# A conditioned residual kernel: other places for two batch-pair products and two rank terms in the order of the output tiles

## The chip, the cores and the metric

The kernel runs on one core of a Trainium2 chip. The metric is the device time of one execution in microseconds, as the median of several runs. A profiled execution is a run of its own: its span goes from the first to the last instruction on the core, and its device time is the span and what lies around it.

## The reference

For each of 8 batches, `x` is a 1024 x 512 matrix and `cond` a vector of 512. Two residual layers follow each other, both with weights that depend on `cond`. Cut to what matters:

```python
h = gelu(layernorm(cond) @ w1 + b1)              # (8, 512)
x_a, x_b = split(h @ w2 + b2)                    # each (8, 512, rank 8)
layer = base_layer[None] + einsum('bdr,bkr->bdk', x_a, x_b)
x = x + (x + einsum('btc,bco->bto', x, layer))   # first layer
ys = cond / sqrt(512)
d = rsqrt(einsum('bi,io->bo', ys * ys, weight * weight) + 1e-8)
x = x + einsum('bsi,io->bso', x * ys[:, None, :], weight) * d[:, None, :]
```

Everything is linear in `x`, so for each batch there is one 512 x 512 matrix Q, and the output is `x[b] @ Q[b]`. With B = base_layer + 2I, and N[b] = I + diag(ys[b]) weight diag(d[b]), Q[b] is B @ N[b] and a term of rank 8 that carries `x_a` and `x_b` through the second layer.

## The kernel before

**Arithmetic.** Each fp32 operand of a large product is split into a high part (a cast on ScalarE) and a low part (a subtraction on VectorE), and each product is done as high x high, high x low and low x high. That is three matmuls for each block of the contraction. An output tile of 128 rows and 512 columns takes 4 x 3 = 12 matmuls.

**Stages.** A set-up stage computes `d` and the low-rank factors, and Q of batches 0 to 3 from the full product B @ N (class `Base`). Then `InOrder.on` is set to False and the main stage begins: 64 output tiles, `main(b, t)` for 8 batches of 8 tiles (L857 to L869). Tile i is tile i % 8 of batch i // 8. Each writes one of four PSUM banks of the pool `po`; ScalarE copies the bank to SBUF (`o`) and issues the output transfer.

**What is interleaved with the tiles.** The Q of batches 4 to 7 is made in the main stage, in two pairs (4, 5) and (6, 7). Class `Pair` makes both batches' B @ N with seven half-size products in the order `ORDER = (1, 2, 5, 6, 3, 7, 4)` (L553), each in two units of six matmuls: 14 units for a pair. The right-hand operands are sums of half matrices n, made by `n_half` (`early`, L592) and split into `nh` and `nl` (`prepare`, L597), two buffers of each. `unit` (L609) issues the six matmuls into a bank and lets ScalarE copy, or VectorE add, the bank into the tiles `q`. Products 1, 5 and 2 take a new bank from the pool `acc`, which has four.

`rank_term(b)` (L512) adds the rank-8 term: four short matmuls (`pr`, 32 rows), each into a bank of `acc` of its own, and four additions on VectorE into `q[b]`. Its operands `fa` and `ft` are read by `load_rank(b)` (L503), eight transfers of 16 KB on POOL's queue, into two buffers each. `split_p(b, j)` (L649) splits a half of Q into `ph` (ScalarE) and `pl` (VectorE); both halves must be there before the tiles of batch b. `load_d(b)` (L325) reads the rows of `d` for a pair into one buffer, by two transfers on POOL's queue.

**What sets the order.** A list `after` holds what is issued behind each tile. `at(b, t, f, ...)` (L825) appends to it; `place(i)` turns a tile number into batch and tile. The number in the two lists of L833 to L855 is thus the tile behind which a step stands. Within a place the order is that of the calls of `at`, so the rank terms of batches 1 to 3 first, then what belongs to pair 4, then to pair 6. Two of the offsets from `first`, the place of a pair's first unit, matter in what follows:

```python
for i in range(2):
    at(*place(first + 2 * n + i), lambda b=b: pairs[b].unit())
...
at(*place(first + 14), rank_term, b)
at(*place(first + 15), rank_term, b + 1)
```

TensorE's matmuls are pinned to the program's order (`mm`, L44). The instructions of VectorE, ScalarE and the queues are not pinned in the main stage, except those of `early`: the tile scheduler orders them when the program is built, by readiness and by their place in the program. [...] Tiles of x (`x_`), their split parts (`xs_`) and the tiles `q` share the nine buffers of the pool `big`; `load_x` is issued by SP.

Of the kernel before, what the change touches and what calls it, by code (L numbers as in the profile page):

```python
# [30 lines left out]
def cond_resid_kernel(ctx: ExitStack, tc: tile.TileContext, small, cond, condrows, consts,  # L31
# [793 lines left out]
    def at(b, t, f, *args):  # L825
        after.setdefault((b, t), []).append((f, args))
# [5 lines left out]
    place = lambda i: divmod(i, NTT)  # L832
    for b in range(1, 4):  # L833
        first = (b - 1) * NTT
        at(*place(max(0, 5 * b - 9)), load_rank, b)
        at(*place(5 * b - 3), rank_term, b)
        for j in range(2):
            at(*place(first + 3 + j), split_p, b, j)
    for b, first in ((4, 14), (6, 29)):

        at(*place(first - 9), load_d, b)
        at(*place(first - 6), new_pair, b)
        for n, p in enumerate(Pair.ORDER):
            at(*place(first - 5 + 2 * n), lambda b=b, p=p: pairs[b].early(p))
            at(*place(first - 2 + 2 * n), lambda b=b, p=p: pairs[b].prepare(p))
            for i in range(2):
                at(*place(first + 2 * n + i), lambda b=b: pairs[b].unit())
        at(*place(first + 2), load_rank, b)
        at(*place(first + 4), load_rank, b + 1)
        at(*place(first + 14), rank_term, b)  # L850
        at(*place(first + 15), rank_term, b + 1)
        at(*place(first + 15), split_p, b, 0)
        at(*place(first + 16), split_p, b, 1)
        at(*place(first + 19), split_p, b + 1, 0)
        at(*place(first + 21), split_p, b + 1, 1)  # L855
# [83 lines left out]
```

## Time and profile before

| | us |
|---|---|
| median of 3 runs | 307.82 |
| lowest and highest run | 307.49, 307.96 |
| the profiled execution, device time | 306.19 |
| its span | 304.4 |
| TensorE busy with matmuls | 296.5 |
| VectorE busy | 177.6 |
| ScalarE busy | 145.5 |
| first output tile's first matmul | 80.80 |
| rank terms of batches 1, 2, 3 | 89.06, 103.36, 117.62 |
| first unit of the first pair | 123.68 |
| rank terms of batches 4, 5 | 181.16, 184.55 |
| first unit of the second pair | 187.50 |
| rank terms of batches 6, 7 | 245.08, 248.47 |

In the lines of the profile PE is TensorE's matmuls, PEld its weight loads, DVE is VectorE, ACT ScalarE, POOL GpSimd, SP the queue that loads x. A tile name stands without its number: `po` is the bank of an output tile, `pp` that of a unit of a pair, `pr` that of a rank term, `q` a Q matrix, `n` a half matrix. Nearly every instruction of VectorE and ScalarE carries line L62 and every matmul L45, those of the helpers, so groups are told apart by tile names. A wait is told as engine, tile, `<-`, and the engine and tile that ended it.

### The profile page before, as it was taken

The page shows a single profiled execution, that of the slowest core. Times are in us where ns is not written, and L with a number is a line of the kernel's source. Part 1 is how long each engine was busy: PE and PEld are TensorE (multiplying, and loading weights), DVE is VectorE, ACT ScalarE, POOL GpSimd, SP SyncE. Part 2 cuts the span into 40 slices and gives each one's busy share as a digit, 9 for nine tenths or more (in the row PEclk, how much of TensorE's full clock was granted, in tenths as well). Part 3 has the DMA queues.
Part 4 walks back from the last instruction along what each step waited for, and adds up shares of the span by engine and source line. Part 5 has one row for each costly group of instructions (what it writes and reads, how often), then busy time and mean ns, then how long its engine had stood idle before and what let it go on. Part 6 is the DMA issues. An engine that isn't in the chain of part 4 may idle for free.

```text
span 304.4 us, 3654 instructions
## 1 busy us (share of the span) xinstructions
PE 296.5 (97%) x1369; PEld 223.4 (73%) x1369; DVE 177.6 (58%) x263; ACT 145.5 (48%) x212; POOL 34.7 (11%) x74
## 2 busy tenths in 40 slices
PE   8999999999999999999999996999999999999995
PEld 3655565467878787888888874888888878888885
DVE  4779840979568599796266429992166186600000
ACT  4756132256466573374554434744555365612221
POOL 0011000057013324200000009000000000000000
PEclk9999999999999999999999999999999999999999
DMA  6999999596519958825151157255151627522222
GB/s 206 409 422 421 410 419 422 207 320 173 182 73 345 329 162 271 272 106 207 71 208 69 62 179 198 65 196 200 69 206 69 206 55 241 225 106 103 87 87 104
DMA packets 19218, 62.11 MB, mean 204 GB/s; under 512 B 2800, under 2 KB 3312, under 8 KB 14848
## 3 DMA queue, kind: packets, MB, share of 16 engines
q1 hardware_dynamic: 6064, 38.78, 35.0%
q10 hardware_dynamic: 9360, 16.78, 14.7%
q0 software_dynamic: 3776, 6.31, 7.6%
q8 instruction: 11, 0.18, 0.2%
q14 instruction: 7, 0.06, 0.1%
HBM read 44.02 MB, written 17.84 MB: 203 GB/s over the span
## 4 chain that ended last, share of the span: by engine, by line
PE 87%; DVE 7%; DMA 4%; ACT 2%; issue 0%; ACTq 0%
PE po L45 57%; PE pp L45 13%; PE pq L45 7%; DMA w<-in_w 4%; PE px L45 3%; DVE n L62 2%; PE warm L45 2%; PE pg L45 2%; DVE q L62 1%; PE pr L45 1%; PE pt_t L45 1%; ACT work L62 1%; DVE scr L62 0%; PE ps_t L45 0%; DVE pl L62 0%
## 5 line engine op out<-in xcount | busy, mean ns | idle before, releaser
L45 PE MATMUL po<-ph,xs 128*128 128x512 f32 (+1 forms) x520 | 164.7, 388 | 0.0
L45 PEld LDWEIGHTS po<-ph,xs 128*128 128x128 f32 x520 | 97.2, 188 | 21.2 <-issue 1.5
L45 PE MATMUL po<-pl,xs 128*128 128x512 f32 (+1 forms) x260 | 100.4, 386 | 0.0
L62 ACT COPY o<-po 128x512 f32<-128x512 f32 (+1 forms) x65 | 37.7, 581 | 86.0 <-PE po L45 86.0
L45 PEld LDWEIGHTS po<-pl,xs 128*128 128x128 f32 x260 | 48.8, 188 | 9.8
L62 DVE TENSOR_TENSOR xs<-x,xs 128x1024 fp32r<-128x1024 f32 x32 | 38.9, 1222 | 20.2 <-ACT xs L62 20.2
L62 ACT CAST xs<-x 128x1024 fp32r<-128x1024 f32 x32 | 33.3, 1052 | 4.8 <-DMA x<-in_x 4.4
L62 DVE TENSOR_TENSOR nl_p<-n,nh_p 128x1024 fp32r<-128x1024 f32 x14 | 17.1, 1224 | 27.5 <-ACT nh_p L62 27.5
L509 POOL DMA_DIRECT2D fa<-kept_a x28 | 13.7, 507 | 86.7 <-PE pr L45 86.6
L62 DVE TENSOR_TENSOR q<-pr,q 128x512 f32<-128x512 f32 x32 | 20.1, 685 | 3.8 <-PE pr L45 3.8
L62 DVE TENSOR_TENSOR pl<-q,ph 128x1024 fp32r<-128x1024 f32 x16 | 19.3, 1221 | 3.2 <-ACT ph L62 3.1
L62 ACT COPY q<-pp 128x512 f32<-128x512 f32 x20 | 11.8, 588 | 17.5 <-PE pp L45 17.5
L45 PE MATMUL pq<-nh,bh 128*128 128x512 f32 x48 | 19.8, 412 | 0.0
L45 PE MATMUL pq<-nl,bh 128*128 128x512 f32 x48 | 19.1, 398 | 0.1
L45 PE MATMUL pq<-nh,bl 128*128 128x512 f32 x48 | 18.9, 395 | 0.0
L62 DVE SCALAR_TENSOR_TENSOR n<-w_sb,ysT,d 128x512 f32<-128x512 f32 x24 | 17.9, 749 | 1.3 <-DMA d<-d_out 1.3
L62 ACT CAST ph<-q 128x1024 fp32r<-128x1024 f32 x16 | 16.6, 1051 | 2.5 <-DVE q L62 2.2
L45 PE MATMUL px<-w,hT 128*32 128x512 f32 x128 | 16.0, 601 | 0.2 <-DMA w<-in_w 0.2
L62 ACT CAST nh_p<-n 128x1024 fp32r<-128x1024 f32 x14 | 14.7, 1052 | 1.6 <-DVE pl L62 0.8
L45 PEld LDWEIGHTS pq<-nh,bh 128*128 128x128 f32 x48 | 9.0, 188 | 8.4 <-issue 5.0
L509 POOL DMA_DIRECT2D ft<-kept_t x28 | 13.8, 515 | 4.9 <-DMA kept_t<-st_t 4.9
L45 PE MATMUL pp<-nh_p,sh 128*128 128x512 f32 x32 | 12.4, 389 | 0.0
(139 smaller groups left out, 286.6 us busy)
## 6 DMA issues: line engine op xcount, KB each, us to landing
w<-in_w SPq DMA_DIRECT2D x16, 1024.0 KB, 10.9
x<-in_x SPq DMA_DIRECT2D x16, 1024.0 KB, 5.3
out<-o ACTq DMA_DIRECT2D x63, 256.0 KB, 2.1
ft<-kept_t POOLq DMA_DIRECT2D x28, 64.0 KB, 2.8
fa<-kept_a POOLq DMA_DIRECT2D x28, 64.0 KB, 2.8
d<-d_out POOLq DMA_DIRECT2D x6, 256.0 KB, 5.7
w_sb<-in_weight SPq DMA_DIRECT2D x2, 512.0 KB, 5.4
b_raw<-in_baseT SPq DMA_DIRECT2D x2, 512.0 KB, 6.2
```

The costliest lines, as they stand in the source:

```text
L45: tc.keep_in_program_order(nc.tensor.matmul(*args, **kw))
L62: return lambda *a, **kw: pin(f(*a, **kw)) if InOrder.on else f(*a, **kw)
L509: nc.gpsimd.dma_start(fold[name, b][32 * c:32 * c + 32, :], kept[name, g][32 * i:32 * i + 32, :])
```

## The change

Four numbers of the schedule are different. Nothing is added or removed.

```diff
     for b in range(1, 4):
         first = (b - 1) * NTT
-        at(*place(max(0, 5 * b - 9)), load_rank, b)
-        at(*place(5 * b - 3), rank_term, b)
+        at(*place(max(0, 4 * b - 8)), load_rank, b)
+        at(*place(4 * b - 2), rank_term, b)
         for j in range(2):
             at(*place(first + 3 + j), split_p, b, j)
-    for b, first in ((4, 14), (6, 29)):
+    for b, first in ((4, 13), (6, 30)):
```

In places (the tile behind which a step stands):

| step | before | after |
|---|---|---|
| `load_rank` of batches 1, 2, 3 | 0, 1, 6 | 0, 0, 4 |
| `rank_term` of batches 1, 2, 3 | 2, 7, 12 | 2, 6, 10 |
| `split_p` of batches 1, 2, 3 | 3 and 4, 11 and 12, 19 and 20 | the same |
| `load_d`, units of the first pair | 5, 14 to 27 | 4, 13 to 26 |
| `load_rank` of batches 4, 5 | 16, 18 | 15, 17 |
| `rank_term` of batches 4, 5 | 28, 29 | 27, 28 |
| `split_p` of batch 4, of batch 5 | 29 and 30, 33 and 35 | 28 and 29, 32 and 34 |
| `load_d`, units of the second pair | 20, 29 to 42 | 21, 30 to 43 |
| `load_rank` of batches 6, 7 | 31, 33 | 32, 34 |
| `rank_term` of batches 6, 7 | 43, 44 | 44, 45 |
| `split_p` of batch 6, of batch 7 | 44 and 45, 48 and 50 | 45 and 46, 49 and 51 |

Batch 4's tiles begin with tile 32, batch 6's with tile 48 and batch 7's with tile 56.

## The prediction

> **What bounds the kernel now.** I read the page first, then who waited for whom, then the chain of waits around the longest wait that TensorE itself has, then busy time by stage.
>
> From the page of the kernel before:
>
> ```profile
> PE 296.5 (97%) x1369; PEld 223.4 (73%) x1369; DVE 177.6 (58%) x263; ACT 145.5 (48%) x212; POOL 34.7 (11%) x74
> ...
> PE   8999999999999999999999996999999999999995
> ...
> PEclk9999999999999999999999999999999999999999
> ```
>
> TensorE is busy 97% of the span at full clock. Of the 40 slices (7.6 us each) one in the middle shows a 6: slice 25, from 182.6 to 190.2 us. There is one hole, and it lies where this change works.
>
> From the table of waits, from 80 us on (who waited, for what, us in total, times, longest):
>
> ```profile
> POOL fa L509 <- PE pr L45: 86.6, 4, 54.9
> ...
> DVE q L62 <- PE pr L45: 3.8, 3, 3.1
> ...
> PEld pp L45 <- DVE q L62: 2.8, 1, 2.8
> PE pp L45 <- DVE q L62: 2.4, 1, 2.4
> ```
>
> In the whole stage of output tiles TensorE waits once: a pair product (`pp`) for an addition into `q` on VectorE, 2.4 us (its weight load 2.8 us). The 86.6 us of POOL are loads queued far ahead; nobody waits for them.
>
> The chain of waits from 176 to 192 us (start, duration, what):
>
> ```profile
> 177.12 1.40 PE pp L45 x6
> 178.51 2.72 PE po L45 x12
> 181.23 0.48 PE pr L45 x2
> 181.71 2.47 DVE q L62 x4
> 184.18 0.66 DVE n L62
> 184.84 1.14 DVE pl L62
> 185.98 0.86 DVE n L62 x2
> 186.84 0.61 DVE q L62
> 187.46 0.04 issue
> 187.50 1.66 PE pp L45 x6
> ```
>
> This is places 27 to 29 of the schedule. `rank_term(4)` stands behind tile 28 and `rank_term(5)` behind tile 29, and the first unit of the second pair stands directly behind `rank_term(5)`. Each rank term takes all four banks of `acc`; the unit needs one back, so it needs the first of batch 5's four additions. That one ends at 187.44, behind four additions of batch 4 and four other VectorE operations, and the unit starts at 187.50.
>
> Busy time of the same stretch, of the corresponding place in the first pair, and of batches 6 and 7 (columns: stretch, length, PE, PEld, DVE, ACT, POOL busy with counts, clock, DMA share, GB/s):
>
> ```profile
> 184.55:187.50 2.95, 0.51 (x6) 0.19 (x5) 2.95 (x6) 1.20 (x2) 2.95 (x7) 1.00 0.77 181
> ...
> 117.62:123.68 6.06, 6.06 (x30) 4.80 (x29) 6.06 (x11) 1.18 (x2) 3.86 (x8) 1.00 0.74 202
> 245.08:257.20 12.12, 12.12 (x57) 9.42 (x57) 9.94 (x14) 7.19 (x9) 0.00 (x0) 1.00 0.47 163
> ```
>
> In the first pair two tiles lie between `rank_term(3)` (117.62) and the first unit (123.68): VectorE is as full there (6.06 of 6.06), and TensorE loses nothing.
>
> [...] here batch 5's first addition starts 2.2 us after its matmul (184.55 to 186.75), though its operands are there, behind others on VectorE. [...]
>
> **The change part by part.** Nothing is added or taken away: the same 1369 matmuls and the same DMAs in another order. So only holes count.
>
> *Second pair, 29 to 30, and the first, 14 to 13 (which also takes its rank terms, loads and splits along).* `rank_term(4)` and `(5)` go behind tiles 27 and 28, the first unit of the second pair behind tile 30. Two whole tiles come between the last rank term and the unit, as in the first pair. Removed is the hole. After an undisturbed rank term the next matmul starts 0.44 us after its first (117.62 to 118.06); here that would be 184.99, and it was 187.50: **2.51 us**. What is late next? The new unit would start at about 187.7 (rank term 4 at 181.16 - 2.72 = 178.44, rank term 5 at 181.8, tiles 29 and 30 end at 187.7). VectorE must have done batch 5's first addition by then. From 179.0, when batch 4's additions can start, there are 8.7 us. Ahead of it could stand: four additions 4 x 0.60 = 2.4; the next n-half 2 x (0.66+0.20) = 1.7; both low halves of batch 4's split 2 x 1.14 = 2.3; one low part of x 1.14; with itself 0.61 that makes 8.2. Even with everything of those places in front it is in time by 0.5; in the order of the trace (2.4 + 2.7 + 0.6) by 3.0. Cost nothing, cover: two tiles of 2.72.
>
> *Between rank terms 4 and 5 there is still one tile.* Batch 5's last rank matmul needs batch 4's last addition: before, 184.18 against about 184.9, 0.7 us to spare. If one 1.22 us operation slid ahead of batch 4's additions it would cost 0.5; no gain is possible. I take 0 and keep 0.5 for the range.
>
> *First pair a tile earlier (first unit from 123.68 to about 120.9).* Its first low part `nl_p` ended at 116.64 and would be wanted at 121.2. VectorE is full from 103.9 to 127.3, so order matters: batch 3's additions (2.4) now come in front of it, but batch 2's (2.4) leave for the idle 3.07 us before 103.89, since `rank_term(2)` moves from 103.36 to about 100.6. These cancel; 4.6 us remain. The second `nl_p` ended at 122.84 and is wanted at 129.4 instead of 132.1. Cost 0, bounded above by 0 while less than 4.6 us slides in front.
>
> *Rank terms 2 and 3 (7 to 6, 12 to 10).* Eight matmuls and eight additions, moved. Banks: batch 1's additions end at 94.6, before 100.6; batch 2's end near 103.5, before batch 3's at 112. Batch 3's banks are free by about 115, the unit comes at 120.9. Their fold tiles: batch 3's eight loads are issued from 89.96 to 93.86 because they wait for `rank_term(1)`, and land 2.8 us later; that is 15 us before 112. Cost 0.
>
> *The loads on POOL's queue.* `load_rank(2)` from place 1 to 0 and `load_rank(3)` from 6 to 4 do not change: both are issued when data or buffer allow (71.7; 89.96). `load_rank(4)` to `(7)` wait for rank terms 2 to 5 and go out 2.7 to 6 us sooner, `load_d(6)` about 3 us sooner. `load_d(4)` now shares place 4 with `load_rank(3)`; before it was issued at 70.5. Were it stuck behind that load, it would be issued at 93.9 and land 7.7 us after its second issue at most, 102.7, and its first reader ran at 107.4, or 104.7 when a tile earlier. So 0 either way. SP's queue: q tiles take their `big` slots a place sooner (13, 19) or later (30, 36). The x parts of the trace are ready 8 us or more before their tile from tile 16 on, longer than one place, 2.72 + 1.36. Cost 0.
>
> *End of the second pair, a tile later.* `rank_term(6)` stays near 245.3 (245.08 + 2.72 - 2.51), but tile 48 starts at 257.17 - 2.51 = 254.66. The low halves of batch 6 ended at 252.76 and 253.89, so now 253.0 and 254.1, and are wanted at 254.9 and 256.2. The margin falls from 4.6 to 1.9 us. Cost 0, with the least cover in the change.
>
> Sum: -2.51 and zeros. Span 304.40 - 2.51 = 301.89; that run lasted 306.19, so 303.68. The median of the runs is 307.82, 1.63 above the profiled one; the same difference gives **305.3 us**, 0.8% faster.
>
> **The rivals.** *Part of the hole stays (306.6).* VectorE's order is the scheduler's, so additions of batch 4 or 5 may sit behind more work; half the hole is 1.25 us, so 307.82 - 1.25. For it: VectorE is full from 181.7 to 191. Against: the first pair shows the new spacing without a hole.
>
> *The wait only moves (307.8).* The backlog of VectorE meets the next product, or the places do not come out as the diff says. Against: the second product's `nl_p` was ready at 181.3, before both rank terms, and the third's at 196.1, 8 us ahead of its unit.
>
> *Slower (309.5), by one mechanism:* batch 6's split is too late for tile 48. At 254.43 ScalarE's queue came out of a wait of 1.84 us for a transfer of x. Were the two casts `ph` of batch 6 (246.94 before) queued behind that and the two casts of x that follow, they would run from 256.9, and the first low half would end at 259.1, wanted at 254.9: 4.2 lost, less 2.5 won, gives +1.7. It decides against the change from 257.4 on, 4.4 us later than I expect. For it: the margin of 1.9. Against: in the trace those casts lie 7.5 us ahead of that wait.
>
> **How the numbers follow.** Full gain 0.77 (305.0 to 305.9: scatter of the runs 0.3 below, the 0.5 above), part 0.08, moved 0.05, slower 0.10. About 0.2%, 0.6 us, is what a measurement of this kernel can tell from no change. The first two cases are faster by more: 0.85; same 0.05; slower 0.10. The range 304.8 to 306.8 holds the first two.
>
> **What would show it.** The table of waits has no TensorE wait for `q` left over 0.5 us, and the middle slice shows a 9. `rank_term(2)` near 100.6, `(3)` near 112, `(4)` near 178.4, `(5)` near 181.8; the second pair's first unit near 187.7; the last matmul near 298.6 (301.1 before). I am wrong if `pp` still waits for `q`, or if `po` of tile 48 waits for `pl` near 254.7.

## The result, and the profile after

| | before | after |
|---|---|---|
| median, us | 307.65 (307.46 to 307.96, 4 runs) | 304.12 (304.07 to 304.17, 4 runs) |
| ratio of the times | | 0.9884, 95% interval 0.9867 to 0.9901 |
| the profiled execution: time, span | 306.19, 304.4 | 304.12, 302.1 |

The kernel is 3.5 us faster, 1.2%. (A fourth run of the kernel before, 307.46, has moved its median from 307.82 to 307.65.) The forecast was 2.5 us, and 304.12 lies 0.7 below the range. The direction and the place were right; the size was not.

The page of the kernel after, with the lines that answer to those of before (busy time by engine; TensorE's busy tenths and granted clock in 40 slices):

```profile
PE 296.5 (98%) x1369; PEld 223.4 (74%) x1369; DVE 177.6 (59%) x263; ACT 145.6 (48%) x212; POOL 34.8 (12%) x74
...
PE   8999999999999999999999999999999999999995
...
PEclk9999999999999999999999999999999999999999
```

The work is the same to a tenth of a microsecond for TensorE and VectorE; the 6 of slice 25 has become a 9. Three lines from the table of waits from 80 us on:

```profile
DVE q L62 <- PE pr L45: 6.6, 3, 4.5
...
DVE q L62 <- PE pp L45: 5.0, 2, 2.5
...
PEld pr L45 <- DVE q L62: 0.7, 2, 0.4
```

The two lines in which `pp` waited for `q` are gone. VectorE's waits for the rank terms have grown from 3.8 to 6.6 us, while TensorE waits for `q` only within the rank terms (0.7 us, as before). The chain of waits from 176 to 193 us runs through TensorE alone:

```profile
178.27 0.43 PE pr L45 x3
178.70 2.99 PE po L45 x12
181.69 0.44 PE pr L45 x2
182.13 5.67 PE po L45 x24
187.80 1.40 PE pp L45 x6
189.20 2.73 PE po L45 x12
```

On this chain, where each piece begins when the one before it ends, the rank terms of batches 4 and 5 stand at 178.27 and 181.69, two whole tiles (5.67 us) follow, and the unit comes at 187.80. Busy time of that stretch and of batches 6 and 7 (columns as before):

```profile
178.27:187.80 9.53, 9.53 (x45) 7.26 (x46) 9.07 (x15) 4.70 (x6) 7.83 (x16) 1.00 0.66 171
245.19:254.70 9.51, 9.51 (x46) 7.25 (x46) 8.87 (x12) 5.76 (x7) 0.00 (x0) 1.00 0.47 186
```

TensorE is busy for all of both. VectorE is still nearly full in the first (9.07 of 9.53): its backlog has not gone, it only has nobody waiting for it.

By the profiles, the start of the last copy (`o`, on ScalarE) moves from 301.11 to 298.43. That is 2.68 us: 0.08 from the set-up and 2.60 from the stage of tiles, where the prediction had 2.51. So the change does in the profile what was forecast. What the profiles don't explain is the time of the other executions: that of before was profiled at 306.19 and runs at 307.65, that of after was profiled at 304.12 and runs at 304.12.

### The profile page after: what moved, and what is told of

The parts are those of the page before. It is cut to its first block, busy times and chain, and to the rows that moved or that the text cites. A ratio compares the mean times of both kernels' runs of the same rounds, so it can differ in the third digit from the quotient of the medians.

```text
span 302.1 us, 3652 instructions
## 1 busy us (share of the span) xinstructions
PE 296.5 (98%) x1369; PEld 223.4 (74%) x1369; DVE 177.6 (59%) x263; ACT 145.6 (48%) x212; POOL 34.8 (12%) x74
## 4 chain that ended last, share of the span: by engine, by line
PE 88%; DVE 5%; DMA 4%; ACT 2%; issue 0%; ACTq 0%
PE po L45 58%; PE pp L45 13%; PE pq L45 7%; DMA w<-in_w 4%; PE px L45 3%; PE warm L45 2%; PE pg L45 2%; DVE n L62 2%; PE pr L45 1%; PE pt_t L45 1%; ACT work L62 1%; DVE scr L62 0%; PE ps_t L45 0%; DVE q L62 0%; PE pq_v L45 0%
```

## The experiments

**The kernel before once more (no edit).** Expected:

> The kernel before, unchanged, to see its spans in the timed runs and a second profile. Theory 1 (the profiled execution of before was an uncommonly short one, and the hole at the second pair costs more in its usual executions): spans near 305.7 us, 1.79 below the times of about 307.6, and a profile of such an execution shows the TensorE wait ahead of the second pair's first unit at 3.5 to 4 us instead of 2.4. Rival (another stage is longer in the usual executions, set-up or tail): the wait stays at 2.4 us and the first output tile begins about 1.3 us later than 80.8, or the end after the last matmul is longer.

Median 307.49, ratio to before 0.9988 (0.9965 to 1.001); the profiled execution took 307.75, with a span of 306.0 and a mean clock of 0.992. Both ideas were wrong. The first tile begins at 80.89, and the wait ahead of the second pair is the same 2.4 us. The difference comes after the wait. Busy time around the hole in this execution (the column after the five engines is the granted TensorE clock):

```profile
184.50:187.40 2.90, 0.48 (x5) 0.16 (x4) 2.90 (x6) 1.17 (x2) 2.87 (x6) 1.00 0.67 171
187.40:189.40 2.00, 1.98 (x7) 1.62 (x8) 2.00 (x5) 0.00 (x0) 1.74 (x4) 0.81 0.71 195
189.40:193.40 4.00, 4.00 (x13) 3.17 (x13) 3.52 (x4) 1.53 (x2) 0.69 (x2) 0.67 0.26 63
193.40:197.50 4.10, 4.10 (x20) 3.37 (x19) 2.83 (x5) 3.23 (x5) 0.00 (x0) 1.00 0.17 64
```

And its chain of waits there:

```profile
186.76 0.61 DVE q L62
...
187.42 1.95 PE pp L45 x6
189.37 4.07 PE po L45 x12
```

The execution profiled first, for comparison: the tile in its chain of waits, and the busy time of the same 4 us.

```profile
189.16 2.73 PE po L45 x12
...
189.40:193.40 4.00, 4.00 (x19) 3.26 (x19) 3.80 (x5) 2.00 (x4) 0.48 (x1) 1.00 0.26 61
```

The unit begins at 187.42, as early as ever, but it and tile 30 take 1.95 and 4.07 us instead of 1.66 and 2.73: 1.63 more. In these 6 us the granted clock is down, 0.81 and 0.67 in the two stretches, and full again after. The clock missing there is 0.19 of 2 us and 0.33 of 4 us, 1.7 us together: as much as 3.4 us at half clock. Single matmuls begin 0.43 us apart there instead of 0.23. "Busy" shows nothing of it: TensorE is busy 4.00 of 4.00 us with 13 matmuls, where the execution profiled first has 19.

The times of the kernel before then fall into two groups. Of its 41 executions timed up to here (these 14 and 27 beside them), 16 had a mean clock of 1.000 and took 305.82 to 306.77; 25 had 0.987 to 0.994 and took 307.33 to 309.31. The execution profiled first, at 306.19 and clock 1.000, was of the first kind. So a second theory: the hole costs itself, and in most executions (25 of these 41) a lower clock follows it for a while.

The later runs had more executions of this kernel beside them. Of 40, 11 had a clock of 1.000 and took 305.87 to 306.44 (median 306.19); 29 had 0.992 to 0.994 and took 307.23 to 308.75 (median 307.68). Of the last 27, 19 were in the upper group. That is 73 of 108 in all. Four of the 73 had a clock of 0.987 and took 308.79 to 309.31, about twice the loss, and none of the four was profiled.

**One part alone.** The second pair:

```diff
-    for b, first in ((4, 14), (6, 29)):
+    for b, first in ((4, 14), (6, 30)):
```

> Only the second pair goes from tile 29 to 30; one tile then lies between the rank term of batch 5 and the first unit. The bank was free 2.9 us after that rank term, a tile is 2.72 and the matmuls of the rank term 0.44, so the hole should be gone. Theory 1 (all of the gain is this hole): 304.1 us, like the full change. Rival (some of the gain comes from the first pair or the early rank terms): between 304.6 and 305.3 us.

304.30 us (304.07 to 304.34), ratio 0.9901 (0.9879 to 0.9923). The first pair:

```diff
-    for b, first in ((4, 14), (6, 29)):
+    for b, first in ((4, 13), (6, 29)):
```

> Only the first pair goes from tile 14 to 13, which takes the rank terms of batches 4 and 5 a tile ahead; the second pair stays at 29. Again one tile lies between the rank term of batch 5 and the unit. Theory 1: 304.1 us, like the full change, since either half of the edit makes the room. Rival (the first pair's earlier place costs something that the second pair's later place pays back, or gains by itself): off 304.1 by 0.5 us or more.

303.98 us (303.76 to 304.33), ratio 0.9893 (0.9869 to 0.9918). The early rank terms:

```diff
-        at(*place(max(0, 5 * b - 9)), load_rank, b)
-        at(*place(5 * b - 3), rank_term, b)
+        at(*place(max(0, 4 * b - 8)), load_rank, b)
+        at(*place(4 * b - 2), rank_term, b)
```

> Only the rank terms of batches 2 and 3 (and their loads) move, to tiles 6 and 10. The hole at the second pair is untouched. Theory 1: 307.6 us, no change. Rival (about 1 us of the gain comes from here): 306.5 us.

Ratio 1.0001 (0.9978 to 1.0024). Its 14 executions lie in the two groups of before, eight from 306.19 to 306.69 and six from 307.61 to 309.16; the median of 306.57 says only that the lower one had eight of fourteen. In the traces of the two kernels with one pair moved, `pp` has no wait for `q`. Either move of a pair alone gives the whole gain, since either puts one tile between the rank term of batch 5 and the unit, and that is enough. The rank terms of batches 2 and 3 give nothing; the wait of 2.4 us is still in that trace.

**The hole filled with work.** If the second theory holds, work that nobody needs must give back the part that went with the clock and leave the wait:

```diff
             bank = self.bank[key]
+            if (b, p, s) == (6, 1, 0):
+                fill = po.tile([P, D], F32, tag="po", name="fill")
+                for _ in range(11):
+                    mm(fill, bh[:, 0, 0:P], bl[:, 0, :], start=True, stop=True)
             self.product(p, s, bank, first)
```

> The kernel before, with eleven matmuls of 512 columns, whose result nobody reads, between the rank term of batch 5 and the first unit of the second pair: 11 x 0.227 = 2.5 us of TensorE work in the 2.4 us of waiting. The unit can't start sooner, so the wait's own 2.5 us stay. Clock theory (the idle hole makes the chip grant half the TensorE clock for 3.4 us afterwards in about half of the executions, 1.6 us more): all executions in one group near 306.1 us, clock 1.000, none near 307.7. Rival (the 1.6 us come from something else in the place of the wait, VectorE or transfers): two groups near 306.1 and 307.7, as before.

The 0.227 us for a matmul are an output tile's 2.72 us over its 12, from the chain of waits of before.

All 17 executions from 305.90 to 306.44, median 306.16, clock 0.998 to 1.000; ratio 0.9962 (0.9949 to 0.9975). The chain of waits:

```profile
184.76 2.78 PE fill L45 x11
187.54 1.40 PE pp L45 x6
```

The unit starts at 187.54, so the time of the wait itself is still paid. Eleven useless matmuls bring the median 1.5 us below that of the kernel with nothing in their place (307.62), to that of its lower group. VectorE and the transfers have the same work as before, so the 1.5 us go with TensorE's idling, and the clock shows the loss gone.

With `range(5)`:

> The same with five such matmuls: TensorE then idles about 1.3 us instead of 2.4, the unit starts at the same time. Clock theory with a threshold[...]: one group near 306.1 us. Rival (any idle microsecond can do it, in proportion): still a second group near 307.7, in a quarter to a half of the executions.

All 17 from 305.91 to 306.66, median 306.16; ratio 0.9967 (0.9953 to 0.9981). The wait of `pp` for `q` in this kernel:

```profile
PE pp L45 <- DVE q L62: 1.1, 1, 1.1
```

A hole of 1.1 us cost no clock in 17 executions (0.998 to 1.000). That there is a threshold was an assumption of mine that no run had shown. With `range(2)`, which left 1.70 us:

> The kernel before with two unread matmuls of 512 columns in the hole: TensorE then waits 2.44 - 0.45 - 0.2 = about 1.8 us (five of them left 1.10). The unit starts at the same time. Theory: [...] two groups, near 306.2 and 307.7 us, some 4 to 6 in 10 of the executions in the upper one. Rival (the bound is nearer to 2.4 us): one group near 306.2.

Median 307.53, ratio 0.9992 (0.9973 to 1.001): 13 of 22 executions in the upper group (307.49 to 308.33, clock 0.992 to 0.994). The share that I expected there was an estimate without a run behind it. With `range(3)`, which left 1.56 us:

> The same with three: the wait is about 1.55 us[...]. Theory: one group near 306.2 us, no loss of clock. Rival (a loss that fades with the length of the hole): a smaller upper group, in 2 to 4 of 10 executions.

Median 306.25, ratio 0.9946 (0.9925 to 0.9967): six of seven in the lower group, but one at 308.05, and that one was profiled. Its busy time:

```profile
184.50:187.50 3.00, 1.70 (x9) 0.68 (x7) 3.00 (x5) 1.51 (x2) 3.00 (x7) 1.00 0.69 168
187.50:189.50 2.00, 1.74 (x4) 1.39 (x5) 2.00 (x5) 0.00 (x0) 2.00 (x5) 0.60 0.79 225
189.50:193.50 4.00, 4.00 (x15) 3.21 (x14) 2.64 (x4) 1.54 (x2) 0.66 (x2) 0.77 0.27 66
```

The clock went down (0.60 and 0.77 in the last two stretches) after a wait of 1.56 us too, for which I had expected no loss. Together, by the length of the wait in the profiled execution: 2.44 us, 29 of 40 executions; 1.70, 13 of 22; 1.56, 1 of 7; 1.10, 0 of 17.

**Where the clock went down.** The record of the granted clock that each trace holds, from which PEclk is made, shows more. In the profile of before its piece at full clock begins 5.69 us after the span's start and is 300.373 us long, 88 times 3.41333; in that of after it begins at 6.02 and is 296.960 us long, 87 times 3.41333. In each of the three traces with the loss one piece at half clock stands behind the hole, 3.413 us long (it begins between 0.1 us before and 1.2 us after the end of the wait). The next table counts stretches of 3.413 us from the start of each record and gives the one with most of the wait in it:

| kernel, wait of `pp` in us | stretch, us | TensorE idle in it, us | clock of the next stretch |
|---|---|---|---|
| early rank terms alone, 2.40 | 183.71 to 187.12 | 2.35 | half |
| kernel before once more, 2.44 | 185.21 to 188.62 | 2.21 | half |
| three unread matmuls, 1.56 | 184.48 to 187.90 | 1.56 | half |
| kernel before as profiled first, 2.44 | 183.18 to 186.60 | 1.54 | full |
| rank term of batch 5 put back (below), 1.41 | 185.98 to 189.39 | 1.41 | full |
| two unread matmuls, 1.70 | 183.07 to 186.48 | 1.02 | full |
| five unread matmuls, 1.10 | 183.61 to 187.03 | 0.58 | full |

In the execution profiled first the end of a stretch at 186.60 cut the 2.44 us into 1.54 and 0.90, and the clock stayed full; in the second profile of the same kernel 2.21 us fell into one, and half clock followed. So an unchanged kernel, with a wait of 2.44 us both times, left traces with and without the loss, as its times lie in two groups. Of this wait 1.56 us in a stretch were followed by half clock and 1.54 by full clock, in one trace each (the ends of matmuls are modelled, so hundredths are not certain). That is what seven traces had, and no rule: at the end of the program stretches with 1.58 us (kernel before) and 1.80 us (two unread matmuls) idle were followed by full clock, and one with 1.93 us (five) by half. What decides it was not shown, nor why 2.44 us lost the clock in 73 of 108 executions and 1.70 us in 13 of 22.

**The rank term of batch 5 put back beside the unit, in the kernel after.**

```diff
-        at(*place(first + 15), rank_term, b + 1)
+        at(*place(first + (17 if b == 4 else 15)), rank_term, b + 1)
```

> The kernel after, with the rank term of batch 5 alone put back directly ahead of the second pair's first unit (behind tile 30), three tiles after that of batch 4. If VectorE's queue made the hole (batch 4's additions and the work around them ahead of batch 5's first addition), the wait shrinks to one addition and what happens to be in front, 0.6 to 1.8 us, with no loss of clock: 304.7 to 305.6 us. If standing next to each other is what costs, the whole hole is back: 306.1 to 307.7 us.

305.70 us (305.48 to 305.89, 8 runs), ratio to the kernel before 0.9951 (0.993 to 0.9973), every clock at 0.997 or more. The trace has a wait again:

```profile
PE pp L45 <- DVE q L62: 1.4, 1, 1.4
```

1.4 us instead of 2.4, and 1.6 us more time than the kernel after, with no loss of clock behind the wait in any of the 8 (the record of this trace is at half clock only from 302.03 on, after the last matmul). Batch 4's additions were long done; what stood ahead of batch 5's first addition was one low half `nl_p` and the end of an n-half. So standing side by side left a wait with batch 4's additions out of the way, and what else stood in VectorE's queue set how long.

**The second pair a tile later still.**

```diff
-    for b, first in ((4, 13), (6, 30)):
+    for b, first in ((4, 13), (6, 31)):
```

> The kernel after, with the second pair a further tile later (31 instead of 30), so that the low halves of batch 6 have one tile less before tile 48. My margin there was 1.9 us after the change; a tile is 2.72, so about 0.8 us would be lost at tile 48: 304.9 us. If the margin was larger than worked out: 304.1 us. If the split also falls behind a transfer of x: over 306 us.

305.47 us (305.07 to 305.85, 7 runs), ratio to the kernel before 0.9936 (0.9915 to 0.9957); 1.35 more than the kernel after. The trace has a wait of tile 48 for the low half:

```profile
PE po L45 <- DVE pl L62: 0.6, 1, 0.6
```

The mechanism of my slower rival exists, without its transfer: `pl` of batch 6 is late. Of 1.15 us by which the last copy is later than in the kernel after, 0.6 are this wait and 0.2 were there from the first tile on (80.93 against 80.72); the rest was not traced.

## Why the prediction was wrong in size

**The place and the cause of the hole: right.** The wait of `pp` for batch 5's first addition was the only one to go, and all four rank terms lie where they were put, by the start of their first matmul: 100.39, 111.97, 178.20 and 181.62 (forecast 100.6, 112, 178.4, 181.8), the unit at 187.64 (187.7). Batch 5's first addition ends at 184.48, 3.2 us ahead of the unit; the forecast had 3.0 in the order of the trace, with 0.60 us from the start of one addition to the next (four took 2.47 us in the chain of before, 0.685 us each).

**The step that failed is the last of the sum: "The median of the runs is 307.82, 1.63 above the profiled one; the same difference gives 305.3".** It took the difference between the profiled execution and the median for something that both kernels have. It belonged to the hole: about 1.5 us of the 1.63 are clock that TensorE lost after it, and the kernel without the hole does not lose them. The profile showed one of the executions that keep their clock (11 of 40 later), and the median stood in the other group. What the runs show in place of it:

| term | us | from |
|---|---|---|
| clock lost after the hole, in the usual execution | 1.49 | 307.68 - 306.19, the two groups of before |
| the hole, with what the end gives back | 2.07 | 306.19 - 304.12 |
| sum | 3.56 | medians of the result: 3.53 |

The sign was in the numbers at hand: three runs within 0.5 us of each other, and a profile 1.3 below the lowest. A distance of that kind is a term to explain, not a constant to carry over.

**The 2.51 us of the hole: right on the chain, 2.07 in time.** The last copy came 2.68 earlier. But from the end of that copy (301.48 before, 298.80 after) to the end of the span it is 2.9 us before and 3.3 after, and outside the span 1.8 and 2.0, so 0.6 is given back. The other kernels with a pair moved end like the kernel after (3.3 to 3.4 us from the last copy), those with the old places like before (2.9 to 3.0). The part outside the span does not go with the pairs: it was 1.73 to 1.88 us with the first pair moved alone, 2.07 to 2.20 with the second, 1.95 to 2.12 with neither, the rank terms alone. What makes either part differ was not settled.

**What I costed at nothing: right.** Rank terms 2 and 3 gave a ratio of 1.0001. The first pair, a tile earlier, cost nothing (303.98 alone). One thing was argued wrongly in the text, without harm: the second product's low half, done before both rank terms in the old order, ends at 189.41 in the new one; it is wanted about 7 us later.

**The least cover, batch 6's low halves: there was more than I said.** I had 253.0 and 254.1 for their ends and 1.9 us to spare. They ended at 249.28 and 252.82, since the scheduler now puts the first ahead of batch 7's additions; the first was wanted at about 254.8. One tile further on the additions of batch 7 did come first, and the first half was late by 0.6 us, near the 0.8 expected.

**The rivals.** No part of the hole stayed, no wait took its place, and tile 48 didn't wait. None of them was on the side where the result fell: I had no case for a hole that costs more than its length. That the result lies no further below the range is luck: 0.6 us were given back at the end, for which the prediction had no term.

## What to carry to other kernels

Price a wait of a busy TensorE by its length and, where executions show a lower clock behind it, by the clock as well: here 2.4 us of waiting cost 2.1, and 1.5 more in the usual execution. Before a change is priced from one profile, ask why its execution differs from the median, and look at the mean clock of several executions; here the spread in two groups, near 306.19 and 307.68, went with the clock, 1.000 and 0.992 to 0.994. Where a step fills all banks of a pool, one tile of other work between it and the next user was enough here, and moving either neighbour gave it.

## What was not expected of the hardware

- A TensorE wait of 2.44 us, in an otherwise full stream of matmuls, was followed by a lower clock in 73 of 108 executions, 1.70 us in 13 of 22, 1.56 in 1 of 7, 1.41 in none of 8, 1.10 in none of 17. The next unit and tile took 1.5 to 1.6 us longer in the three executions with the loss that were profiled.
- In the three traces with the loss it was one stretch of 3.413 us at half clock, behind a stretch in which TensorE idled for 1.56, 2.21 or 2.35 us; in the four others of the table, with 1.54, 1.41, 1.02 and 0.58 us, the clock stayed full.
- A halved clock did not show as idle time: TensorE was busy 4.00 of 4.00 us with 13 matmuls in place of 19, at a clock of 0.67 in place of 1.00.
- Eleven matmuls into a bank that nobody reads, in a wait whose end stayed where it was, took 1.5 us off the median (307.62 to 306.16).
- The end of the program after the last copy was 0.4 us longer in every kernel with a moved pair, 3.3 to 3.4 against 2.9 to 3.0 us, and remained unexplained.
